# Layer 3 of a four-layer network: the shared expert's output held aside, the gathers taken by quarters, and the side work beside the first half's experts traced at twice the pace

## The chip, the cores and the metric

The kernel runs on one core of one Trainium2 chip. The metric is the time of one execution in microseconds (us). Profiles come from the hardware profiler; its engines are PE (TensorE matmul), PEld (TensorE weight load), DVE (VectorE), ACT (ScalarE), POOL (GpSimd) and SP (SyncE, which here only starts DMAs). Lines such as L1305 are line numbers of the kernel before.

## The reference

A network of four layers works on `x` of shape 4 x 1024 x 128 in fp32. Every layer is a mixer and a feed-forward part, each with a residual and a layer norm:

```python
x = _layernorm(x + _L3_attn_ref(x, ...), axis=-1)
x = _layernorm(x + _L3_ffn_ref(x, ...), axis=-1)
return x
```

Layers 0 to 2 (a gated scan and a quantized linear, a state space model and 16 experts, causal attention and 8 low-rank experts) are not touched. In layer 3 the mixer is a gated unit whose Toeplitz product runs over the first axis of `x`, which is 4 long, so a token mixes only with the tokens at the same place of the other three sequences. The feed-forward part of layer 3 is what this case is about:

```python
scores = softmax(flat @ router_w.T + router_bias)          # 32 experts
topk_scores, topk_idx = top_k(scores, 4)
topk_scores = topk_scores / clip(topk_scores.sum(-1), 1e-12)
h = silu(flat @ gate_w[e]) * (flat @ up_w[e])              # 128 wide, each expert e
sel = (h @ down_w[e])                                      # the four chosen experts
out = (sel * topk_scores).sum(1)
out = out + (silu(flat @ sgate_w.T) * (flat @ sup_w.T)) @ sdown_w.T   # shared, 512 wide
```

The shared expert reads the same input as the routed ones, and both sums are added to that input before the last norm.

## The kernel before

**Layout and parts.** `x` stays in SBUF as 32 tiles of 128 tokens x 128 features. Time is cut into four quarters; a quarter is 8 tiles (two of each of the 4 sequences). Layer 3 works on three parts: a is the quarters 0 and 1 (16 tiles), b is quarter 2, c is quarter 3 (8 tiles each). `xT` holds the same tokens turned, with features on the partitions.

**The chain of one part.** `l3_attn` (L1556) is the mixer: projections on PE, SiLU on ACT, the Toeplitz steps on DVE, the norm, and at its end `xT`. `l3_route` (L1656) computes the logits, the top 4 and the weights, a long row of small DVE steps; `positions` (L1239) turns them into a place in a list sorted by expert (`posl3a`, `posl3b`, `posl3c`, made at L1280) and the experts of the list's tiles. `spread` (L1317) is the **scatter**: for each tile of tokens four indirect DMAs, issued by POOL at L1305, write the rows of `x` into the list in HBM (`l3ra`, `l3rb`, `l3rc`): 64 for a, 32 for b, 32 for c. `l3_shared` (L1677) is the shared expert: per block of four tiles it makes four GLU chunks (two matmuls of `xT`, SiLU, product) and the down projection, and then DVE adds the result from PSUM to `x` at L1693. Part a has four blocks, b and c two each.

`small_experts` (L1705) runs the routed experts over the sorted list in groups of four list tiles, 20 groups for a and 12 each for b and c. A group is: a load `xg` by SP (L1336), which waits for all scatters of the part; PE transposes into `tp`; gate and up matmuls `gu` with the weights of the tile's expert; SiLU on ACT (L1735); the product `hg` on DVE (L1736); transposes and a DVE copy to `hT` (L169); the down matmuls; a copy `yg` from PSUM on ACT (L1750); and a store by SP to the list of outputs (`l3ya`, `l3yb`, `l3yc`). After the last group stands a branch (`rest_of`, L1358) for lists that are longer than the planned size; every engine passes it, and with this input its body is skipped.

`collect` (L1385) is the **gather**: for each tile of tokens four indirect DMAs (again POOL at L1305) fetch the outputs of its four experts into a buffer `yt`, and DVE adds them, weighted, to `x` (L1396). `yt` has 8 buffers of one tile, so the ninth tile's gather waits for the adds of the first. `finish` (L1788) norms a quarter (L185) and stores it with four DMAs of SP. The last part goes through `close` (L1863), which does this two tiles at a time.

**What orders the work.** Engines take their instructions in the order in which the program was traced, and the order is written by hand with generators in `all` (L1874). `chain` runs generators in turn, `abreast` side by side by their listed costs. `mix(main, side, pace)` (L241) traces a step of the main work, then as much of the side work as its cost allows; the side's instructions are put behind the main ones on their engine:

```python
            due += got[0]
            while due > 0.0:
                took = self.queued(side)
                due = 0.0 if took is None else due - took[0] * pace
```

So a pace of 0.75 lets the side advance by 1/0.75 of the main work's listed time. `press` (L1850) traces the side alone until a name is listed. The shared expert may not write to `x` before the part's scatter has read it, so `l3_shared` asserts that the scatter is listed. The end of the kernel (L1925 to L1945) makes one side chain `on`, in which the mixer and route of b, the scatter of b, the gathers and norms of a, the mixer and route of c, the scatter of c and the gathers and norm of b follow, and beside it:

```python
self.run(self.mix(self.chain(self.l3_shared(a, sw), self.l3_experts(a, wall3)), on, 0.75, False))
self.press(on, listed("l3b"))
self.run(self.mix(self.chain(self.l3_shared(b, sw), self.l3_experts(b, wall3)), on, 0.75, False))
self.press(on, listed("l3c"))
self.run(self.mix(self.chain(self.l3_shared(c, sw), self.l3_experts(c, wall3)), on))
self.run(self.close(c, yp))
```

In POOL's order this gives: the branch behind the experts of a, 32 scatters of b, 64 gathers of a, the branch behind the experts of b, 32 scatters of c, 32 gathers of b, the branch behind the experts of c, 32 gathers of c.

Of the kernel before, what the change touches and what calls it, by code (L numbers as in the profile page):

```python
# [20 lines left out]
P = 128  # L21
# [48 lines left out]
def tile_of(b, i):  # L70

    return i // 2 * QT + b * 2 + i % 2


class Kernel:
# [1598 lines left out]
            yield from self.positions(cp, "l3" + part.name, mask, w, part.nt, E3, K3)  # L1674
            yield (10.0,)

    def l3_shared(self, part, sw):  # L1677

        nc, x = self.nc, self.x
        NC = FS3 // P  # L1680
        with ExitStack() as c2:
            hp = self.pool(c2, "l3sh" + part.name, 2)
            ps = self.pool(c2, "l3sp" + part.name, 2, space=PSUM)
            assert "l3" + part.name in self.listed
            wd = sw[:, 2, :].rearrange("p (c d) -> p c d", d=D)
            for blk in range(part.t0 // 4, (part.t0 + part.nt) // 4):
                h = self.tile(hp, [P, NC, BLK], "hs", bufs=1)
                for c in range(NC):
                    f = slice(c * P, (c + 1) * P)
                    self.glu(ps, hp, h[:, c, :], sw[:, 0, f], sw[:, 1, f], blk)  # L1690
                py = self.down(ps, h, wd, NC)
                s = slice(blk * 4, blk * 4 + 4)
                nc.vector.tensor_tensor(x[:, s, :], py, x[:, s, :], ALU.add)  # L1693
                yield (9.0,)

    def l3_wall(self, ctx, right=False):
# [88 lines left out]
    def l3_experts(self, part, wall):  # L1785
        return self.small_experts("l3", E3, part, wall)

    def finish(self, part):  # L1788

        for q in range(part.q0, part.q0 + part.nq):  # L1790
            self.norm(self.quarter(q))
            yield (5.0,)
            for b in range(B):
                t = tile_of(b, 2 * q)
                self.nc.sync.dma_start(
                    out=self.out[b, q * TQ : (q + 1) * TQ, :].rearrange("(k p) d -> p k d", p=P),
                    in_=self.x[:, t : t + 2, :],
                )
            yield (1.0,)

    def chain(self, *gens):
        for g in gens:
# [53 lines left out]
        yield from self.l2_route(part)  # L1856
        yield from self.spread("l2", part, K2)

    def last(self, part, yp):
        yield from self.collect("l3", part, K3, yp)  # L1860
        yield from self.finish(part)

    def close(self, part, yp):  # L1863

# [9 lines left out]
    def all(self):  # L1874
# [4 lines left out]
        with ExitStack() as ctx:  # L1879
            lgp = self.pool(ctx, "l2lg")  # L1880
            self.l2_lg = self.tile(lgp, [P, NT, E2], "lg")
            with ExitStack() as early:

                self.l0_setup(early)
                self.l2_wr = self.load(lgp, self.ins["l2_wr"])
                self.run(self.l0_attn((0, 1)))
                self.l1_setup()
                self.l2_setup()
                self.zero_lists("l1")
                self.run(self.l0_ffn((0, 1)))  # L1890
                self.run(self.l1_attn((0, 1)))

                self.run(self.l1_route(a))
                self.run(self.mix(self.l0_attn((2, 3), True), self.spread("l1", a, K1)))
                self.zero_lists("l2", "l3")
                with ExitStack() as c2:
                    wall = self.l1_wall(c2)
                    yp = self.pool(c2, "l1ya", 5, right=True)
                    side = self.chain(self.l0_ffn((2, 3), True), self.l1_attn((2, 3), True))
                    self.run(self.mix(self.chain(self.l1_shared(a), self.l1_experts(a, wall)), side, 2.0, False))  # L1900
                    self.run(self.mix(self.abreast(self.l2_weights(), side), self.l1_close(a, yp)))
            with ExitStack() as c2:
                wall = self.l1_wall(c2)
                self.run(self.mix(self.l2_attn(0), self.chain(self.l1_route(r), self.spread("l1", r, K1))))
                wall2 = self.l2_wall(c2)
                yp = self.pool(c2, "l1yr", 5, right=True)
                self.run(self.mix(self.chain(self.l1_experts(r, wall), self.l1_shared(r)), self.routed(a2)))
                self.run(self.mix(self.l2_experts(a2, wall2), self.l1_close(r, yp)))
            listed = lambda name: lambda: name in self.listed
            on = self.served(  # L1910
                self.chain(self.rows_in(a2), self.onward(a, True)),
                (lambda: self.rows_done >= B + 2, self.routed(m2)),
                (lambda: self.rows_done == 2 * B, self.routed(n2)),
            )
            self.run(self.mix(self.l2_attn(1), on, drain=False))
            with ExitStack() as c3:
                with ExitStack() as c2:
                    wall = self.l2_wall(c2)
                    self.press(on, listed("l2m"))
                    self.run(self.mix(self.l2_experts(m2, wall), on, drain=False))  # L1920
                    self.press(on, lambda: {"l2n", "routed l3a"} <= self.listed)
                    sw, wall3 = self.l3_wall(c3, True)
                    on = self.chain(on, self.rows_in(m2))
                    self.run(self.mix(self.l2_experts(n2, wall), on, drain=False))
                self.press(on, listed("l3a"))  # L1925
                yp = self.pool(c3, "l3y", 8)

                on = self.chain(
                    on, self.collect("l2", n2, K2, yp, which=(0, 1, 4, 5)),
                    self.abreast(  # L1930
                        self.chain(self.l3_attn(b), self.l3_route(b)),
                        self.collect("l2", n2, K2, yp, which=(2, 3, 6, 7)),
                    ),
                    self.abreast(
                        self.chain(self.spread("l3", b, K3), self.when(listed("made l3a")), self.last(a, yp)),
                        self.chain(self.l3_attn(c), self.l3_route(c)),
                    ),
                    self.spread("l3", c, K3), self.when(listed("made l3b")), self.last(b, yp),
                )
                self.run(self.mix(self.chain(self.l3_shared(a, sw), self.l3_experts(a, wall3)), on, 0.75, False))  # L1940
                self.press(on, listed("l3b"))
                self.run(self.mix(self.chain(self.l3_shared(b, sw), self.l3_experts(b, wall3)), on, 0.75, False))
                self.press(on, listed("l3c"))
                self.run(self.mix(self.chain(self.l3_shared(c, sw), self.l3_experts(c, wall3)), on))
                self.run(self.close(c, yp))  # L1945
        bad = self.nc.values_load(self.flag[0:1, 0:1], min_val=0, max_val=1)
        with self.tc.If(bad > 0):  # L1947
            with ExitStack() as ctx:
# [9 lines left out]
                for p in self.parts:  # L1958
                    self.run(self.onward(p))
                    with ExitStack() as c2:  # L1960
                        sw, wall = self.l3_wall(c2)
                        self.run(self.l3_shared(p, sw), self.l3_experts(p, wall))
                        self.run(self.last(p, self.pool(c2, "l3y" + p.name, 5)))


@with_exitstack
# [162 lines left out]
```

## Time and profile before

| what | value |
|---|---|
| runs | 2449.0, 2435.38, 2435.16, 2447.52, 2448.98 us; median 2447.52 |
| the profiled execution | 2442.41 us, its span 2440.6 us |
| busy PE, PEld | 1603.6 us (66%), 955.2 us (39%) |
| busy DVE, ACT | 1270.5 us (52%), 803.3 us (33%) |
| busy POOL | 768.3 us (31%) |
| DMA | 187.10 MB, mean 77 GB/s |
| queue q0, which carries the indirect DMAs | 42.86 MB, 5.6% of the DMA engines' time |
| mean granted TensorE clock | 0.821 |

The span is the time from the first to the last record of the profiled execution; all stamps below are us from its start. Busy times are sums over the whole span, and they are far from full on every engine, so they do not say what sets the end. For that one cuts the span into stretches and looks at what each engine does in each. Layer 3's experts fill the last fifth: the experts of a begin at about 1942, and the last record is at 2440.6. A row of a group of instructions reads: line, engine, operation, output <- inputs, count, then the shortest, mean and longest duration in ns or the busy time, and the first and last start.

### The profile page before, as it was taken

The numbers are of one execution on the slowest core, as the hardware profiler recorded it, in microseconds if no ns is written. First come the engines' busy times: TensorE is split into PE (matmuls) and PEld (weight loads), VectorE is DVE, ScalarE is ACT, GpSimd is POOL, SyncE is SP. The second block draws the span as 40 slices with busy tenths as digits, with TensorE's granted clock in tenths as the row PEclk, the third lists the DMA queues.
The fourth block names the chain that finished last, engine by engine and source line by source line (L and its number), as shares of the span: only waits on it lengthen the run. The fifth ranks groups of instructions, "written<-read, shape, count | busy, mean of one in ns | idle before, by whom it ended". The sixth has DMA issues, their size and how long they took to land. (4 is left out here: it accounts for less than half of the span.)

```text
span 2440.6 us, 27065 instructions
## 1 busy us (share of the span) xinstructions
PE 1603.6 (66%) x9017; PEld 955.2 (39%) x9017; DVE 1270.5 (52%) x3630; ACT 803.3 (33%) x1159; POOL 768.3 (31%) x701
## 2 busy tenths in 40 slices
PE   7535776976571675586969787877726798262480
PEld 3214433843230335544623232344514485152270
DVE  8767795655670564324535675473602275252352
ACT  5511372322240332222336564542201164030140
POOL 5531285145227002234132002002372102727504
PEclk9766788988785898888979998888868899686695
DMA  9930002334201014312130000021411141131232
GB/s 308 288 104 0 12 36 80 117 110 152 77 28 52 17 57 155 100 50 62 43 104 21 1 1 17 2 113 39 159 71 33 43 123 53 51 99 61 67 100 59
DMA packets 215530, 187.10 MB, mean 77 GB/s; under 512 B 16528, under 2 KB 194064, under 8 KB 214864
## 3 DMA queue, kind: packets, MB, share of 16 engines
q1 hardware_dynamic: 194672, 142.29, 18.4%
q0 software_dynamic: 20704, 42.86, 5.6%
q8 instruction: 84, 1.38, 0.2%
q14 instruction: 70, 0.57, 0.1%
HBM read 88.49 MB, written 96.60 MB: 76 GB/s over the span
## 5 line engine op out<-in xcount | busy, mean ns | idle before, releaser
L1059 ACT ACTIVATE pr<-sc 128x1024 f32<-128x1024 f32 x288 | 279.6, 1021 | 321.5 <-PE sc L157 189.7
L157 PE MATMUL sc<-qm,kT 32*128 32x512 f32 (+3 forms) x1536 | 198.2, 559 | 21.7 <-ACT pr L1059 21.4
L157 PE MATMUL gu<-ld,xgT 128*128 x640 | 167.5, 406 | 60.1 <-issue 36.2
L157 PE MATMUL s<-pr,va 128*32 128x512 f32 (+3 forms) x1536 | 175.1, 523 | 46.1 <-issue 26.3
L165 PE MATMUL tp<-ld,hg 128*128 128x128 f32 x624 | 100.5, 282 | 102.5 <-DVE hg L1736 36.7
L157 PE MATMUL gu<-wall,xgT 128*128 x304 | 155.4, 637 | 2.9 <-ACT xgT L167 2.0
L157 PEld LDWEIGHTS gu<-ld,xgT 128*128 128x128 f32 x640 | 121.5, 201 | 86.3 <-issue 45.5
L1065 DVE TENSOR_TENSOR pr<-pr,ld 128x512 f32<-128x512 f32 (+1 forms) x160 | 92.1, 580 | 104.8 <-ACT pr L1059 101.7
L169 DVE COPY hT<-tp 128x512 f32<-128x512 f32 x118 | 80.8, 685 | 122.6 <-remote 64.8
L165 PEld LDWEIGHTS tp<-ld,hg 128*128 128x128 f32 x624 | 79.0, 145 | 155.4 <-issue 58.7
L157 PEld LDWEIGHTS sc<-qm,kT 32*128 32x128 f32 x1536 | 85.2, 198 | 120.5 <-issue 66.3
L1736 DVE TENSOR_TENSOR hg<-sg,gu 128x256 f32<-128x256 f32 x160 | 65.6, 416 | 127.9 <-ACT sg L1735 107.0
L167 ACT COPY xgT<-tp 128x512 f32<-128x512 f32 x99 | 57.9, 586 | 220.1 <-PE tp L165 155.2
L1305 POOL DMA_INDIRECT l1ra<-x,posl1a x64 | 93.3, 1458 | 61.2 <-DVE posl1a L1280 42.0
L1502 ACT ACTIVATE sg<-gu 128x512 f32<-128x512 f32 x76 | 45.4, 598 | 198.7 <-PE gu L157 126.0
L165 PE MATMUL tp<-ld,xg 128*128 128x128 f32 x396 | 65.0, 292 | 67.4 <-ACT hT L167 26.0
L1735 ACT ACTIVATE sg<-gu 128x256 f32<-128x256 f32 x160 | 60.8, 384 | 140.2 <-PE gu L157 69.0
L1305 POOL DMA_INDIRECT yt<-l1yr,posl1r x64 | 60.6, 947 | 142.8 <-DVE x L1396 83.2
L157 PEld LDWEIGHTS s<-pr,va 128*32 128x32 f32 x1536 | 38.6, 112 | 154.7 <-issue 108.0
L1504 DVE TENSOR_TENSOR hg<-sg,gu 128x512 f32<-128x512 f32 x76 | 51.7, 681 | 82.7 <-ACT sg L1502 65.0
L1305 POOL DMA_INDIRECT l1rr<-x,posl1r x64 | 62.2, 972 | 96.8 <-DVE posl1r L1280 77.6
L1305 POOL DMA_INDIRECT yt<-l1ya,posl1a x64 | 69.8, 1091 | 70.2 <-DVE x L1396 29.6
(441 smaller groups left out, 3516.1 us busy)
## 6 DMA issues: line engine op xcount, KB each, us to landing
wall<-wall SPq DMA_DIRECT2D x16, 768.0 KB
l3ra<-zero SPq DMA_DIRECT2D x1, 6144.0 KB
ld<-in_l_w SPq DMA_DIRECT2D x2, 3072.0 KB
wall<-we SPq DMA_DIRECT2D x24, 256.0 KB
ld<-in_l_w SPq DMA_DIRECT2D x1, 6144.0 KB
l1ra<-zero SPq DMA_DIRECT2D x1, 5120.0 KB
l1rr<-zero SPq DMA_DIRECT2D x1, 5120.0 KB
xg<-l3ra SPq DMA_DIRECT2D x20, 256.0 KB
```

What stands on the lines that cost most here:

```text
L157: return self.nc.tensor.matmul(out, lhsT, rhs, start=start, stop=stop)
L165: nc.tensor.transpose(pt[:, k * P : (k + 1) * P], s, self.ident)
L167: nc.scalar.copy(dst, pt[:, : n * P])
L169: nc.vector.tensor_copy(dst, pt[:, : n * P])
L1059: nc.scalar.activation(pr, sc[h], AF.Exp)
L1065: nc.vector.tensor_tensor(d, d, cst["tril"].unsqueeze(1).unsqueeze(1).to_broadcast([P, 2, n, P]), ALU.mult)
L1305: ins = self.nc.gpsimd.indirect_dma_start(**kw)
L1502: nc.scalar.activation(sg, gu[:, 0, :], AF.Silu)
L1504: nc.vector.tensor_tensor(h, sg, gu[:, 1, :], ALU.mult)
L1735: nc.scalar.activation(sg, pg[:, :, 0, :], AF.Silu)
L1736: nc.vector.tensor_tensor(h[:, 2 * c : 2 * c + 2, :], sg, pg[:, :, 1, :], ALU.mult)
```

## The change

- **Shared output held.** For b and c, `l3_shared` gets a tile `sh` of 8 x 128 columns. ACT copies each block's result from PSUM into it, and the add to `x` is one DVE instruction over all 1024 columns, traced after the experts of the part. Since `x` is not written before that, the shared expert may stand ahead of the scatter: it now starts when the mixer's `xT` is listed (`mixed l3b`, `mixed l3c`), with the rest of the route and the scatter traced beside it, and only the experts wait for the scatter to be listed.
- **Gathers by quarters.** `finish` and `last` take one quarter. The gathers and the norm of a's first quarter stay beside the mixer and route of c; those of its second quarter move behind the scatter of c, ahead of the gathers of b.
- **Pace.** Beside the shared expert and experts of a the pace goes from 0.75 to 0.5, so the side advances by 2 units per unit of the main work. Beside the experts of c it goes from 1 to 0.75; what is left of the side is traced at the end of that, as before.

The gathers of c and `close` stay as they are. `l3_shared` for a still adds each block to `x` at once. The number of indirect DMAs and the matmuls are the same. In POOL's order the change gives: 12 scatters of b, the branch behind the experts of a, 20 scatters of b, 32 gathers of a, the branch behind the experts of b, 32 scatters of c, 32 gathers of a, the branch behind the experts of c, 32 gathers of b, 32 gathers of c.

```diff
--- before.py
+++ after.py
@@ -1674,14 +1674,18 @@
             yield from self.positions(cp, "l3" + part.name, mask, w, part.nt, E3, K3)
             yield (10.0,)
 
-    def l3_shared(self, part, sw):
+    def mark(self, name):
+        self.listed.add(name)
+        yield (0.0,)
+
+    def l3_shared(self, part, sw, sh=None):
 
         nc, x = self.nc, self.x
         NC = FS3 // P
         with ExitStack() as c2:
             hp = self.pool(c2, "l3sh" + part.name, 2)
             ps = self.pool(c2, "l3sp" + part.name, 2, space=PSUM)
-            assert "l3" + part.name in self.listed
+            assert sh is not None or "l3" + part.name in self.listed
             wd = sw[:, 2, :].rearrange("p (c d) -> p c d", d=D)
             for blk in range(part.t0 // 4, (part.t0 + part.nt) // 4):
                 h = self.tile(hp, [P, NC, BLK], "hs", bufs=1)
@@ -1689,8 +1693,12 @@
                     f = slice(c * P, (c + 1) * P)
                     self.glu(ps, hp, h[:, c, :], sw[:, 0, f], sw[:, 1, f], blk)
                 py = self.down(ps, h, wd, NC)
-                s = slice(blk * 4, blk * 4 + 4)
-                nc.vector.tensor_tensor(x[:, s, :], py, x[:, s, :], ALU.add)
+                if sh is None:
+                    s = slice(blk * 4, blk * 4 + 4)
+                    nc.vector.tensor_tensor(x[:, s, :], py, x[:, s, :], ALU.add)
+                else:
+                    t = blk * 4 - part.t0
+                    nc.scalar.copy(sh[:, t : t + 4, :], py)
                 yield (9.0,)
 
     def l3_wall(self, ctx, right=False):
@@ -1785,18 +1793,17 @@
     def l3_experts(self, part, wall):
         return self.small_experts("l3", E3, part, wall)
 
-    def finish(self, part):
-
-        for q in range(part.q0, part.q0 + part.nq):
-            self.norm(self.quarter(q))
-            yield (5.0,)
-            for b in range(B):
-                t = tile_of(b, 2 * q)
-                self.nc.sync.dma_start(
-                    out=self.out[b, q * TQ : (q + 1) * TQ, :].rearrange("(k p) d -> p k d", p=P),
-                    in_=self.x[:, t : t + 2, :],
-                )
-            yield (1.0,)
+    def finish(self, q):
+
+        self.norm(self.quarter(q))
+        yield (5.0,)
+        for b in range(B):
+            t = tile_of(b, 2 * q)
+            self.nc.sync.dma_start(
+                out=self.out[b, q * TQ : (q + 1) * TQ, :].rearrange("(k p) d -> p k d", p=P),
+                in_=self.x[:, t : t + 2, :],
+            )
+        yield (1.0,)
 
     def chain(self, *gens):
         for g in gens:
@@ -1856,9 +1863,10 @@
         yield from self.l2_route(part)
         yield from self.spread("l2", part, K2)
 
-    def last(self, part, yp):
-        yield from self.collect("l3", part, K3, yp)
-        yield from self.finish(part)
+    def last(self, part, yp, q=0):
+
+        yield from self.collect("l3", part, K3, yp, q * QT, QT)
+        yield from self.finish(part.q0 + q)
 
     def close(self, part, yp):
 
@@ -1928,20 +1936,25 @@
                 on = self.chain(
                     on, self.collect("l2", n2, K2, yp, which=(0, 1, 4, 5)),
                     self.abreast(
-                        self.chain(self.l3_attn(b), self.l3_route(b)),
+                        self.chain(self.l3_attn(b), self.mark("mixed l3b"), self.l3_route(b)),
                         self.collect("l2", n2, K2, yp, which=(2, 3, 6, 7)),
                     ),
                     self.abreast(
-                        self.chain(self.spread("l3", b, K3), self.when(listed("made l3a")), self.last(a, yp)),
-                        self.chain(self.l3_attn(c), self.l3_route(c)),
+                        self.chain(self.spread("l3", b, K3), self.when(listed("made l3a")), self.last(a, yp, 0)),
+                        self.chain(self.l3_attn(c), self.mark("mixed l3c"), self.l3_route(c)),
                     ),
-                    self.spread("l3", c, K3), self.when(listed("made l3b")), self.last(b, yp),
+                    self.spread("l3", c, K3), self.last(a, yp, 1), self.when(listed("made l3b")), self.last(b, yp),
                 )
-                self.run(self.mix(self.chain(self.l3_shared(a, sw), self.l3_experts(a, wall3)), on, 0.75, False))
-                self.press(on, listed("l3b"))
-                self.run(self.mix(self.chain(self.l3_shared(b, sw), self.l3_experts(b, wall3)), on, 0.75, False))
-                self.press(on, listed("l3c"))
-                self.run(self.mix(self.chain(self.l3_shared(c, sw), self.l3_experts(c, wall3)), on))
+                self.run(self.mix(self.chain(self.l3_shared(a, sw), self.l3_experts(a, wall3)), on, 0.5, False))
+                hold = self.pool(c3, "l3hold", 2)
+                for p in (b, c):
+                    self.press(on, listed("mixed l3" + p.name))
+                    sh = self.tile(hold, [P, QT, D], "sh")
+                    self.run(self.mix(self.l3_shared(p, sw, sh), on, 0.75, False))
+                    self.press(on, listed("l3" + p.name))
+                    self.run(self.mix(self.l3_experts(p, wall3), on, 0.75, p is c))
+                    s = slice(p.t0, p.t0 + QT)
+                    self.nc.vector.tensor_tensor(self.x[:, s, :], sh, self.x[:, s, :], ALU.add)
                 self.run(self.close(c, yp))
         bad = self.nc.values_load(self.flag[0:1, 0:1], min_val=0, max_val=1)
         with self.tc.If(bad > 0):
```

The slow general path behind a flag, which isn't taken here, calls `last` once for each quarter.

## The prediction

> **What bounds the kernel now.** I read the slices of the page first. In the last quarter the TensorE digits fall to 1 and 2 where POOL's are 5 to 7. So I asked for the busy times of the stages of layer 3, in this order: experts of part a; shared and scatter of b; experts of b; shared of c; experts of c; the close. Columns: stretch, length, then busy time and count of PE, PEld, DVE, ACT, POOL, then granted clock, DMA share, GB/s.
>
> ```profile
> 1942.00:2041.00 99.00, 89.59 (x560) 76.90 (x560) 64.28 (x208) 63.40 (x128) 0.00 (x0) 0.98 0.35 106
> 2041.00:2146.00 105.00, 43.45 (x143) 25.13 (x143) 34.27 (x104) 11.84 (x20) 62.98 (x64) 0.69 0.16 49
> 2146.00:2273.00 127.00, 60.57 (x331) 51.58 (x331) 54.39 (x207) 33.41 (x65) 62.26 (x64) 0.72 0.27 81
> 2273.00:2334.00 61.00, 30.06 (x96) 15.65 (x96) 15.27 (x59) 9.12 (x13) 30.35 (x32) 0.67 0.22 60
> 2334.00:2384.00 50.00, 45.55 (x288) 40.55 (x288) 30.00 (x93) 26.87 (x52) 0.00 (x0) 0.97 0.41 125
> 2384.00:2440.00 56.00, 0.00 (x0) 0.00 (x0) 16.85 (x60) 1.44 (x5) 30.18 (x32) 0.51 0.19 52
> ```
>
> Where POOL has no indirect DMA, PE is busy for 90% of the time. In the three stages with indirect DMAs it is busy for 41 to 49%, and no other engine is full. The views of the tiles give POOL's order there (first and last start):
>
> ```profile
> L1305 POOL DMA_INDIRECT l3rb<-x,posl3b x32: 954/958/1949, 2053.2 to 2094.4; - x32
> L1305 POOL DMA_INDIRECT yt<-l3ya,posl3a x64: 938/944/1086, 2095.6 to 2216.4; - x64
> L1305 POOL DMA_INDIRECT l3rc<-x,posl3c x32: 954/958/1761, 2217.6 to 2257.9; - x32
> L1305 POOL DMA_INDIRECT yt<-l3yb,posl3b x32: 940/944/1014, 2274.9 to 2313.8; - x32
> L1336 SPq DMA_DIRECT2D xg<-l3rc x12: 359/360/501, 2331.2 to 2363.2; - x12
> L1305 POOL DMA_INDIRECT yt<-l3yc,posl3c x32: 940/944/947, 2386.7 to 2425.4; - x32
> ```
>
> Part c's scatter stands behind all 64 gathers of a, though its positions (`posl3c`, L1280) were made at 2205.2. The waits of 2095 to 2145 show what a burst of indirect DMAs does:
>
> ```profile
> DVE x L1693 <- remote: 47.7, 1, 47.7
> PEld s L157 <- issue: 30.8, 13, 2.6
> PE s L157 <- issue: 30.7, 14, 2.5
> ```
>
> PE waits for nothing that the profile shows, yet starts one matmul in 2.5 us; DVE stands for 47.7 us at an add whose matmuls ended at 2103. By 20 us slices, 2120 to 2140 has 8 matmuls and no DVE or ACT instruction, 2300 to 2320 two and none. So back-to-back indirect DMAs stop the other engines. They don't stop at once: PE went on for 19 us after the start of the burst at 2053.2, 15 after 2274.9, 12 after 1886.6. I call this the grace. After a burst ends it takes 5.6 us (2314.7 to 2320.3) until DVE goes on. When POOL's gathers are spaced by waits, as between 2162 and 2189, PE keeps working. **The tail is therefore POOL's bursts and the experts mostly in turn**, and what counts is their order. The view of the DMAs from 2095 to 2145 lists no packet of the two instruction queues; the cause of the stop it doesn't tell.
>
> [...]
>
> **The change, part by part.** All times are on the clock of the profiled execution (span 2440.6, 1.8 us around it, 2442.4 in all; the runs shown have a median of 2447.5, 5 above it). The instructions of the changed program, engine by engine, give POOL's new order: 12 scatters of b, the branch after experts a, 20 scatters of b, 32 gathers of a's first quarter, scatter c, 32 gathers of a's second quarter, gathers of b, gathers of c. The number of indirect DMAs is the same.
>
> *Pace 0.5 beside experts a.* Route b's positions now come with three expert groups of a left; before, they came at 2052.2, after all. DVE takes on the rest of route b and the start of c's attention, some 20 us of work (2039 to 2060 in the trace, with other work between). It had 35 us free of 99, and PE gets only some 2 us more. So the stage, 2040.4 at its end, grows by 0 to 20; I take 7, nearer the row with free time: 2047. With 4.9 us a group (98 us for 20), the first scatter starts at 2047 - 15 + 1 = 2033, 20 earlier. The last groups of a (14 us) fit into the grace, and their lists are in memory by 2048, long before the gathers of a start at 2074.
>
> *First burst.* 64 indirect DMAs took 82.2 us (2053.2 to 2135.4): now 2033 to 2115. Shared b had 8 us ahead of the burst and the grace; now it starts 14 us into the burst. In the stopped part (2072 to 2139) PE got 54 matmuls through; shared b has 96, so some 30 are left for after it, 6 us more than before. The first transposes of experts b came 11.3 us after the burst (2146.7); now 2115 + 11 + 6 gives 2132, and I take 2133 (2126 if shared b is done, 2146 if half of its 21 us is left).
>
> *Shared output held.* L1693 on b and c, four adds of 0.69 us on DVE, becomes four ACT copies (0.59 each, as L1750) and two adds of 1024 columns (L1957); no row has this form, and by two of 0.69 each they cost 2.8 in all, the same (0 to 6). ACT is idle there. The add for b waits for all scatters of b; behind it on DVE stand c's toeplitz steps and the products of experts b, which need those scatters anyway. What goes is the stall of L1693 on scatter b (11.7 us), inside the burst: nothing by itself.
>
> *Experts b without a burst.* Before, 8 of 12 groups took 42 us (2147 to 2189) beside c's attention, its route and spaced gathers: 5.3 each. Now all 12 run so: 64 us, to 2197 (43 us if each took 3.54 as in experts c, so 2176; 78 at 6.5, so 2211). POOL is idle meanwhile. Positions of c come just after the branch behind experts b, so scatter c starts at 2201, not 2217.7.
>
> *Scatter c and second half of a.* 41.2 us, to 2242. Five of the eight tile buffers are free by then, so 20 gathers follow without a pause, 25 us, to 2267. Restart 5.6: 2273. Shared c runs beside this as it did beside the gathers of b: it got as far as the middle of its second block in the grace, and 9.5 us were left (2321.7 to 2331.2). So it ends at 2283, and 3 us later (xg issue to first transposes, 2331.2 to 2334.2) experts c start at 2286; before, 2334.2. If the grace covers it, 2279. On SP's queue four stores of a's quarter now stand between the third and the fourth load for experts c; they wait for a's norm, which DVE does ahead of the first products anyway: 0, up to 5.
>
> *Experts c.* 48 us (2334.2 to 2382.0), to 2334. The eight gathers left of a take 10 us, in the grace. DVE adds a's 32 rows between, as it added b's before: same cover.
>
> *Gathers of b, what is late next.* They were over at 2314.7, 72 us before they could matter. Now each tile waits for an add of a, the first behind 7 groups: 2286 + 4 + 7 x 3.54 = 2315. 32 gathers take 39.8 us: 2355, and a pause for the last buffers, 6 (0 to 26, if the last groups of experts c fall outside the grace): 2361. The gathers of c follow. From their first start to the end of the span was 2440.6 - 2386.7 = 53.9.
>
> **Sum:** 2361 + 54 = 2415 of span, 25 less than 2440.6 (rounded); with the 1.8, **2417**. Low end: experts a not longer (-7), shared b done in the burst (-6), experts b at 4.4 a group (-11), shared c in the grace (-7), no pause (-6): 2380. High end: experts a +13, experts b +14, pause +16: 2460.
>
> **Rivals.**
> 1. *Larger gain.* The grace starts anew in POOL's small pauses, so shared b and c and the ends of experts b and c lose little. For it: from 2162 to 2189, with 13 indirect DMAs, PE was busy for 24 of 27 us. Against: the bursts at 2223 and 2290 stopped all. Half of the low end's terms: 2399; all: 2380.
> 2. *The first half's pace gives nothing.* Experts a drag by 20 us, since the long chain of route b stands in DVE's order ahead of the products, and experts b take 6.5 a group. Then only the new place of scatter c pays: 2417 + 13 + 14 = 2444.
> 3. *Slower: no grace, strict turns.* For it: PE stopped at 2190.5, 8 us after 12 gathers began at 2182.7. Scatter b then stops experts a with three groups left: scatter to 2074, restart and groups to 2094, gathers to 2134, restart and shared b (two blocks of 10.4, 1919.3 to 1929.8 in shared a) to 2161, experts b 2164 to 2228, scatter c and 20 gathers from 2231 to 2297, restart and shared c to 2324, the eight gathers and a restart to 2343, experts c to 2391, gathers of b, no longer out of the way, to 2431, end 2485: 2487. It decides once the gathers of c start after 2399, 12 us later than before.
>
> **How the numbers follow.** Forecast (2402 to 2430) 0.46; larger gain (2370 to 2402) 0.18; rival 2 (2430 to 2454) 0.22; slower 0.14. A measurement of this kernel can tell about 0.5%, 12 us, from no change. Faster by more: 0.46 + 0.18 = 0.64; within: 0.22; slower by more: 0.14. The range 2380 to 2460 leaves out some 0.07 below and 0.12 above.
>
> **What would show it.** First l3rb scatter at 2033; first transposes of experts b near 2133, of experts c near 2286; `posl3c` near 2200; gathers of b inside experts c; gathers of c from 2361. If experts a end after 2060, the first step is wrong; if experts b take 78 us, the fourth; if PE works through the 66 us from scatter c on, my reading of the bursts is. A first gather of c after 2387 means that nothing was won.

## The result and the profile after

The changed kernel took 2455.76 us (median of 42 runs, 2436.43 to 2469.71), the kernel before 2443.54 us (median of 79). The ratio is 1.0046, 95% interval [1.0033, 1.0059]: slower by 11 to 12 us, less than the 0.5% that the text on record called the limit of one measurement, but clear of zero over so many runs. The forecast was 2417 us, a gain of 25.

The profiled execution took 2471.81 us (span 2469.8), 16 above the median of the runs. First the busy times of its stretches of layer 3, cut where its own stages change (columns as before: stretch, length, then busy time and count of PE, PEld, DVE, ACT, POOL, clock, DMA share, GB/s):

```profile
2080.00:2098.00 18.00, 0.00 (x0) 0.00 (x0) 0.00 (x0) 0.58 (x1) 11.39 (x13) 0.50 0.16 57
2098.00:2135.00 37.00, 13.53 (x20) 4.95 (x20) 2.07 (x3) 5.02 (x7) 27.24 (x29) 0.59 0.20 54
2135.00:2160.00 25.00, 21.88 (x89) 13.55 (x90) 11.92 (x27) 5.72 (x10) 0.00 (x0) 0.80 0.00 1
2160.00:2220.00 60.00, 56.56 (x356) 48.20 (x354) 41.73 (x142) 35.37 (x69) 0.00 (x0) 0.97 0.32 98
2225.00:2306.00 81.00, 28.93 (x97) 17.40 (x95) 16.38 (x53) 5.36 (x9) 61.39 (x64) 0.65 0.16 51
2316.00:2350.00 34.00, 30.38 (x183) 27.04 (x184) 15.81 (x37) 18.52 (x36) 0.00 (x0) 0.90 0.50 147
2350.00:2380.00 30.00, 11.94 (x67) 10.38 (x65) 8.40 (x26) 2.92 (x7) 22.73 (x24) 0.72 0.26 69
2404.00:2470.00 66.00, 0.00 (x0) 0.00 (x0) 26.52 (x102) 1.48 (x5) 30.63 (x32) 0.50 0.20 56
```

The stretches are cut at the ends of the bursts, and they alternate: where POOL has its indirect DMAs PE has 0 to 40% of the time, where POOL has none PE has 88 to 94%. (In the last stretch PE has no work left.) The experts of b (2160 to 2220) now run without an indirect DMA beside them and take 60 us. The views of the tiles of the same kernel give POOL's order:

```profile
L1305 POOL DMA_INDIRECT l3rb<-x,posl3b x32: 954/958/1236, 2050.0 to 2089.8; - x32
L1305 POOL DMA_INDIRECT yt<-l3ya,posl3a x64: 940/944/1030, 2094.0 to 2305.5; - x64
L1305 POOL DMA_INDIRECT l3rc<-x,posl3c x32: 954/958/1479, 2225.4 to 2265.4; - x32
L1305 POOL DMA_INDIRECT yt<-l3yb,posl3b x32: 940/944/1097, 2350.2 to 2402.8; - x32
L1305 POOL DMA_INDIRECT yt<-l3yc,posl3c x32: 940/944/1047, 2404.1 to 2443.3; - x32
```

The gathers of c begin at 2404.1; in the kernel before they began at 2386.7. The waits of 2060 to 2135 (engine, tile and line, releaser: us in all, times, longest) show what stands still beside scatter b and the first gathers:

```profile
PE s L165 <- issue: 35.2, 2, 21.6
DVE hs L744 <- remote: 29.5, 1, 29.5
ACT yg L1758 <- remote: 15.1, 1, 15.1
```

`yg` at L1758 is a group of the experts of a: its last two stores, which the forecast had inside the grace, left at 2072.1 and 2090.6, while scatter b ran from 2050.0 to 2089.8.

### The profile page after: what moved, and what is told of

It is laid out like the page before. It is cut to its first block, busy times and chain, and to the rows that moved or that the text cites. A ratio compares the mean times of both kernels' runs of the same rounds, so it can differ in the third digit from the quotient of the medians.

```text
span 2469.8 us, 27062 instructions
## 1 busy us (share of the span) xinstructions
PE 1606.3 (65%) x9017; PEld 957.8 (39%) x9017; DVE 1274.5 (52%) x3628; ACT 804.0 (33%) x1161; POOL 769.1 (31%) x701
## 5 line engine op out<-in xcount | busy, mean ns | idle before, releaser
L744 DVE TENSOR_TENSOR hs<-sg,pu 128x512 f32<-128x512 f32 x48 | 32.7, 685 | 121.9 <-remote 74.0
L165 PEld LDWEIGHTS tp<-ld,xg 128*128 128x128 f32 x396 | 49.8, 152 | 115.5 <-issue 48.2
```

Of the source, the lines that this page charges most:

```text
L165: nc.tensor.transpose(pt[:, k * P : (k + 1) * P], s, self.ident)
L744: nc.vector.tensor_tensor(dst, sg, pu, ALU.mult)
```

## The experiments

The runs fell on different chips, and these are of two kinds. On the first kind, that of the result, the kernel before takes 2430 to 2444 us; on the second it takes 2032 to 2036. Ratios are against the kernel before on the same chip. On the second kind the kernel before has times but no profile. In a stretch where POOL has nothing to do the two kinds run alike: from the first to the last store of the experts of a the kernel before takes 84.6 us on the first kind, and the quarters alone, the same program up to there, 84.6 on the second. All kernels of this table compute the same thing as the kernel before.

| kernel | first kind: ratio, interval | second kind: ratio, interval |
|---|---|---|
| the whole change | 1.0046 [1.0033, 1.0059]; again 1.0037 [1.0018, 1.0056] | 0.9945 [0.9922, 0.9968] |
| pace 0.5 alone | 1.0008 [0.9988, 1.0028] | 0.9915 [0.9897, 0.9934] |
| quarters alone | 1.0032 [1.0013, 1.0050] | 0.9939 [0.9914, 0.9963] |
| held output alone | 1.0010 [0.9982, 1.0038] | 1.0221 [1.0203, 1.0239] |
| held and quarters, pace 0.75 | not run | 1.0357 [1.0339, 1.0375] |
| before, spaced by 512 columns | 0.9712 [0.9670, 0.9754] | not run |
| before, spaced by 128 columns | not run | 1.0075 [1.0047, 1.0103] |
| pace 0.5, spaced by 512 | not run | 1.0216 [1.0181, 1.0252] |
| whole change, spaced by 512 | not run | 1.0203 [1.0172, 1.0234]; again 1.0198 [1.0160, 1.0236] |
| whole change, spaced by 128 | not run | 0.9994 [0.9978, 1.0011] |
| before, all layers spaced by 320 | not run | 1.0332 [1.0297, 1.0367] |

### One part at a time, second kind of chip

Edits: the pace alone (`0.75` to `0.5` in the line of the experts of a); the quarters alone (`finish`, `last` and the side chain of the change, the shared output added at once); the held output alone (`sh`, `mark` and the loop over b and c, with `self.last(a, yp, 0), self.last(a, yp, 1)` in one place; the loop brings the pace of 0.75 beside the experts of c with it); all but the pace of 0.5.

> The kernel before with one edit: the pace beside the shared expert and experts of a is 0.5. Theory A (the loss of the whole change comes from the dragged end of the experts of a, whose last groups fall into the burst of scatter b): last store of l3ya near 2090 instead of 2041, first transposes of the experts of b near 2162 instead of 2147, and a time 10 to 20 us above that of the kernel before. Theory B (the loss comes from the gathers of b that now stand ahead of those of c): the pace alone costs nothing, within 5 us of the kernel before.

> The kernel before with the gathers of a in two quarters, the second behind the scatter of c, at the old pace of 0.75 and 1; the shared output is added at once as before. Theory A: the first transposes of the experts of b stay near 2147, the experts of b take about 60 us, the scatter of c starts near 2210; gathers of b stop the last groups of the experts of c, so what was won is given back: within 7 us of the kernel before. Theory B: 10 us or more slower than the kernel before.

> The kernel before with the shared output of b and c held and added after the experts, the shared expert starting when the mixer's part is done; all gathers of a in one piece as before, pace 0.75 beside the experts of a. Theory A: shared b gains its 8 us ahead of the scatter at most, shared c runs beside the scatter of c and not beside the gathers of b, and the experts of c start when the gathers of b are over, near 2320 instead of 2334: 8 to 16 us faster than the kernel before. Theory B says nothing against it; if the held tile and its late add cost by themselves, it is no faster.

> The changed kernel with the pace beside the experts of a back at 0.75. Theory A: the experts of a end near 2041 again, the experts of b start 12 to 16 us earlier than in the changed kernel, and the time is 10 to 20 us below it, at or a little below the kernel before. Theory B: as slow as the changed kernel, 8 to 16 us above the kernel before.

The time of 2033 us came unlooked for, and theories A and B, whose numbers were for the first kind, both miss here. The pace and the quarters gained 0.85% and 0.6%, the held output lost 2.2%, and with the quarters 3.6%. Of the waits of the last kernel from scatter b to the end of the experts of b (1765 to 1913) these bear on the loss:

```profile
ACT sg L1743 <- PE gu L157: 44.8, 14, 27.7
DVE x L1396 <- DMA yt<-l3ya,posl3a: 30.9, 4, 28.4
DVE x L1957 <- DMA l3rb<-x,posl3b: 30.5, 1, 30.5
```

The add of the held output, written after the experts, stands on DVE ahead of their products, and waits 30.5 us for the scatters of b. That wait ends at 1808.1, when the list of the experts of b is complete, so it holds back c's mixer, which stands behind it, and not the experts. Inside the experts DVE then waits 28.4 us, to 1848.8, at an add of a gathered tile that stands ahead of their next products. The experts of b took 100 us there instead of the 65 of the quarters alone. At the pace of 0.75 shared b, which now goes first, also pushes route b back: `posl3b` comes 242 us after `posl3a`, with the quarters alone 231. The held output alone has the same two waits (30.5 and 28.5 us).

### The change and the kernel before, profiled side by side; a measuring block

> The changed kernel as it is, on the chip of the experiments, where the kernel before takes 2033 us and not 2444. If the held output is what costs there (the kernels with it took 1.022 and 1.036 of the time before, those without it 0.992 and 0.994), 1.02 to 1.04; if the pace of 0.5 and the held output need one another, 0.98 to 1.00.

> The kernel before, for its profile on the chip of the experiments. If the difference of 400 us comes from bursts of indirect DMAs that do not stop the other engines here, PE, DVE and ACT go on at more than half their pace in the stretches of scatter b and of the gathers of a and b, and stretches without indirect DMAs take as long as before.

> The kernel before with a measuring block behind its last store, outputs unchanged: first DVE, ACT and PE streams without waits and 40 turns of DVE and ACT with no indirect DMA; then the streams beside a burst of 64 gathers; then the turns beside such a burst; then the turns beside 64 gathers with a memset of 512 columns on POOL between them. Where bursts stop the others by slow signals between engines, the streams run at full pace in the second part and a turn takes 5 us or more in the third; where by instruction supply, the streams slow down too; where they do not stop them, all parts but for a few per cent take as long as the first. The fourth shows whether spacing changes it.

These three fell on a chip of the first kind. The changed kernel gave 1.0037 and a second profile (span 2446.5), nearer to its median than the first. The kernel before gave a span of 2444.1, with the stages of its first profile within 5 us. In the probe (streams are instructions without waits, a turn is one DVE instruction and one of ACT that wait for each other) the scheduler moved the turns ahead: 66 of the 120 had run before the second burst, 54 ran beside it, and the spaced burst had nothing beside it, so it says nothing. The busy times of the first stretch (streams, no DMA) and of the second (the same streams beside 64 gathers, after its first 9 us):

```profile
2431.00:2446.00 15.00, 15.00 (x117) 15.00 (x118) 15.00 (x146) 14.58 (x100) 0.00 (x0) 0.87 0.04 12
2465.00:2537.00 72.00, 11.30 (x31) 8.14 (x30) 11.43 (x61) 6.83 (x40) 54.31 (x59) 0.53 0.18 52
```

```profile
L157 PE MATMUL pm<-src x31: 270/371/565, 2464.8 to 2536.0; 128*128 128x128 f32 x31
L157 PEld LDWEIGHTS pm<-src x30: 186/288/288, 2465.1 to 2533.9; 128*128 128x128 f32 x30
  issue: 121.2, 58
```

Without indirect DMAs PE, DVE and ACT are full, with 117 matmuls in 15 us; beside them PE does 31 in 72 us. The last row is PE's idle time, matmuls and weight loads together: 58 waits, none of them for anything that the profile names. So for these streams a burst of indirect DMAs is neither a late signal nor a late transfer of their data: they start instructions more slowly. The text on record had asked for this if the supply of instructions is what suffers, but the probe doesn't tell that from any other cause of slow starts. Beside the second burst 54 turns of DVE and ACT, all that were left, went through in its first 36 us. So here too the stop did not come at once; how long this grace would have lasted is not known.

### One part at a time, first kind of chip

> The pace of 0.5 alone again, for a chip where the kernel before takes 2440 us. Theory C (indirect DMAs in a burst and the other engines work strictly in turn there, so that only their sum and the waits between them count): the scatter of b starts some 20 us earlier, the last two groups of the experts of a are stopped until it ends, the experts of b start near 2147 as before, and the time stays within 6 us of the kernel before. Theory A: 10 to 20 us slower.

> The quarters alone again, for a chip where the kernel before takes 2440 us. Theory C: the experts of b end near 2208 instead of 2271, but the gathers of b leave the stretch beside shared c and stop the last five groups of the experts of c; shared c stands behind a burst of 72 indirect DMAs and one of 32 follows inside the experts of c: 15 to 35 us slower than the kernel before. If the gathers are covered by the experts, faster by 10 us or more.

> The held shared output alone again, for a chip where the kernel before takes 2440 us. Theory C: shared c is done before the gathers of b, which stand in a burst as before, so the experts of c start near 2320 instead of 2334: 5 to 15 us faster than the kernel before. If the late add, which waits on DVE for all scatters of b, holds up what stands behind it (as on the other chip, where it waited 30.5 us and the kernel was 1.022 of the time before): 10 us or more slower.

Theory C got the pace right, and the direction of the quarters, not their size (7 us instead of 15 to 35). The held output gained nothing, where theory C had 5 to 15 us. All four kernels have moved the middle of the stage and not the first gather of c. Times in us after `posl3a` was made, which takes out what the layers ahead vary by:

| kernel | first scatter of b | first load for experts b | first scatter of c | first load for experts c | first gather of c | end |
|---|---|---|---|---|---|---|
| before | 313 | 404 | 478 | 591 | 647 | 701 |
| pace alone | 292 | 404 | 484 | 586 | 644 | 698 |
| quarters alone | 311 | 401 | 451 | 566 | 650 | 704 |
| held alone | 324 | 367 | 497 | 565 | 646 | 699 |
| whole change (second profile) | 295 | 404 | 469 | 559 | 648 | 713 |

The first load for the experts of c comes 5 to 32 us earlier than before, the first gather of c within 3 us of that of the kernel before in all. From there to the end each part alone takes 54 us, as before, and the whole change 65. The held output alone shows how it is lost, in its stretches from scatter c to the end of the experts of c:

```profile
2233.00:2302.00 69.00, 23.01 (x89) 12.67 (x87) 24.17 (x82) 6.24 (x10) 42.26 (x38) 0.69 0.12 43
2302.00:2335.00 33.00, 14.21 (x56) 10.97 (x56) 2.70 (x6) 4.96 (x9) 24.87 (x27) 0.71 0.36 103
2335.00:2382.00 47.00, 36.16 (x232) 32.87 (x232) 27.66 (x88) 22.27 (x43) 0.48 (x1) 0.86 0.35 105
```

The experts of c have their list at 2302, but the gathers of b run until 2335 and PE does 56 matmuls beside them; the other 232 follow in 47 us. In these kernels, on this kind of chip, bursts and matmuls work mostly in turn, and putting one ahead of the other moved nothing.

### Spacing the DMAs

```python
         self.moved = self.moved[-130:] + [ins.ins.name]
+        if self.spaced:
+            f = self.nc.gpsimd.memset(self.fill, 0.0)
+            self.tc.add_manual_dep(f.ins, ins.ins.name, behind, reason="queued behind")
+            self.moved.append(f.ins.name)
```

> The kernel before with a memset of 512 columns on POOL behind each indirect DMA of this last stage but for the gathers of c: one DMA in 1.66 us instead of 1.25. It computes the same. If the others stop because a queue fills up at one DMA in 1.25 us and drains a little more slowly, spacing sets them free: the experts of b start near 2110 instead of 2147, those of c near 2300 instead of 2334, and the time falls by 20 to 40 us. If each indirect DMA costs the others a fixed time, nothing is won and the bursts take 0.4 us more for each of 160: 20 to 60 us slower.

It took 2360.05 us against 2429.64: 0.9712 [0.9670, 0.9754], and more than the 20 to 40 us that were expected. So the stop hangs on how closely the DMAs follow one another and is no fixed cost of each; what stops the engines this doesn't tell. Two of its tiles, its stretches, and one of the kernel before (the last row):

```profile
L1306 POOL DMA_INDIRECT l3rb<-x,posl3b x32: 964/965/1276, 2016.1 to 2069.7; - x32
L1306 POOL DMA_INDIRECT yt<-l3yc,posl3c x32: 940/944/1003, 2305.8 to 2344.5; - x32
```

```profile
2072.00:2120.00 48.00, 40.27 (x242) 35.09 (x242) 30.96 (x118) 25.84 (x51) 43.28 (x59) 0.90 0.49 138
2120.00:2140.00 20.00, 0.00 (x0) 0.00 (x0) 0.00 (x0) 0.00 (x0) 18.05 (x25) 0.57 0.19 56
...
2235.00:2290.00 55.00, 39.18 (x224) 34.26 (x224) 23.42 (x67) 19.37 (x40) 48.29 (x64) 0.81 0.46 130
```

```profile
2275.00:2315.00 40.00, 18.97 (x57) 8.95 (x55) 9.54 (x43) 7.33 (x10) 30.27 (x32) 0.67 0.29 78
```

From 2072 to 2120 POOL issues some 29 DMAs and as many memsets, and PE is busy for 40 of 48 us beside them; before, at 1.25 us a DMA, PE was busy for 19 of the 40 us beside the gathers of b, most of them in the grace. 32 scatters take 55 us instead of 42, yet the first gather of c comes 573 us after `posl3a` instead of 647. Some 30 of these 74 us are won ahead of scatter b, since the edit also spaces the last gathers of layer 2, beside shared a: the first store of the experts of a comes 187 us after `posl3a` instead of 217. What is left are waits that the profile can name: from 2120 to 2140 all but POOL stand still behind one add on DVE, which waits 24.6 us for gathers of a.

> The changed kernel with the same memset of 512 columns behind each indirect DMA but those of the gathers of c. It computes the same. Theory C (only the stops took the gain of the change): with the stops gone the change shows its worth, and this is faster than the spaced kernel before, under 2350 us where that took 2360. Theory D (the change costs by itself: the held add waits on DVE for all scatters of b with the products of the experts queued behind it, and the gathers of b stand between the experts of c and the gathers of c): 2375 to 2430 us.

> The pace of 0.5 alone, with the spacing. With the stops gone the earlier route of b should pay as it did on the chip without stops (0.992 of the time before): about 2340 us. If the dragged experts of a cost as much as the earlier scatter wins: 2360.

> The kernel before with a memset of only 128 columns behind each indirect DMA, about 1.35 us a DMA. If the stops follow from a queue that drains a little more slowly than one DMA in 1.25 us, this is between: 2380 to 2430 us, with a longer run of work before each stop. If any pause on POOL's queue sets the others free, 2355 or less, since it costs less than the longer memset.

> The kernel before with a memset of 320 columns behind each indirect DMA of all layers but the gathers of c. If the bursts of layers 1 to 3 ahead of the last stage stop the other engines too (between 1780 and 1825 PE has no or few matmuls beside the scatter of a): 20 to 60 us faster than the 2360 of the kernel spaced in the last stage alone. If those bursts stand alone on the path, 0.3 us for each of them is lost: 2360 to 2420.

These fell on the second kind, so they don't answer what was asked of the first. There the spaced forms are slower, the more so the longer the pause: 0.75% for 128 columns (1.35 us a DMA by the estimate on record), 2.0 to 2.2% for 1.67 us with the change or the pace, 3.3% in all layers. Whether 128 columns are enough on the first kind, and whether layers 1 and 2 gain from spacing there, is open.

> The changed kernel with the memset of 512 columns behind each indirect DMA, again, for a chip where the kernel before takes 2440 us; there the kernel before with the same spacing took 0.971 of the time before. Theory C (only the stops took the gain of the change): under 0.967. Theory D (the change costs by itself, as on the chip without stops, where its spaced form took 1.020): 0.98 to 1.00.

> The changed kernel as it is, beside it. On a chip where the kernel before takes 2440 us: 1.004 again. On one where it takes 2033 us, theory D: 1.01 to 1.03, since the held output without the pace took 1.036 there; theory C: below 0.99, since nothing stops the other engines there.

> The changed kernel with a memset of 128 columns behind each indirect DMA but those of the gathers of c: one DMA in 1.35 us. On a chip where the kernel before takes 2440 us, if a rate a little below one DMA in 1.26 us sets the other engines free and the change has its worth there as on the chip without stops (0.9945 of the time before): 2350 to 2385 us, the experts of b without a gap and no stretch of 10 us without an instruction of PE; if 1.35 us is still too fast, the stops stay and the time is 2400 to 2450. On a chip where it takes 2033 us: between the changed kernel without spacing (0.9945) and with the larger memset (1.020), 1.00 to 1.01, by 160 times 0.08 us of POOL time.

Again the second kind. The changed kernel as it is took 0.9945 there: it is worth 0.55% where bursts don't stop the others, less than the pace alone (0.9915, on another chip of that kind). That is less than theory C asked for (below 0.99) and the other sign from theory D. With the pace of 0.5 the add of the held output (L1957) starts at 1776.2, after the scatter of b (1732.1 to 1772.4), DVE stands 0.3 us ahead of it instead of 30.5, and no add of a gathered tile holds DVE up in the experts of b. So the price of the held output hangs on the pace beside it. Its stretches of scatter b, experts b, scatter c, experts c, gathers of b and gathers of c:

```profile
1732.00:1774.00 42.00, 35.53 (x152) 22.43 (x151) 24.27 (x72) 18.94 (x34) 32.11 (x33) 0.88 0.24 84
1774.00:1837.00 63.00, 58.54 (x370) 49.97 (x369) 44.64 (x153) 35.84 (x69) 32.77 (x32) 0.97 0.48 132
1841.00:1883.00 42.00, 21.95 (x96) 13.51 (x94) 15.62 (x53) 7.53 (x12) 31.99 (x33) 0.78 0.13 50
1883.00:1935.00 52.00, 45.97 (x288) 41.13 (x288) 30.35 (x86) 25.09 (x50) 39.59 (x41) 0.92 0.64 177
1935.00:1964.00 29.00, 0.00 (x0) 0.00 (x0) 16.01 (x63) 2.35 (x3) 21.91 (x24) 0.52 0.33 84
1964.00:2018.00 54.00, 0.00 (x0) 0.00 (x0) 19.58 (x73) 1.48 (x5) 30.07 (x32) 0.50 0.23 61
```

Beside 33 unspaced scatters 152 matmuls go through, and beside 41 unspaced gathers the experts of c do all their 288. From scatter c on POOL is the bound here: from the first scatter of c at 1841.3 to the last gather of c at 2003.5 it issues 128 DMAs in 162 us, one in 1.27 us, and the experts of c are done 29 us before the gathers of b. That is the place where a transfer that was out of the way before now stands on the path. With the larger memset the same queue took 200 us (1854.3 to 2054.1), 38 us more, and the first scatter of c came 336 us after `posl3a` instead of 323; together that is about what the spaced form of the change loses against it (2.6%). With 128 columns the gain and the loss cancelled.

## Why the prediction was wrong

The reading of the bottleneck held: bursts and the other engines work mostly in turn. What failed is that the forecast still let work overlap the bursts, shared b in the first one and the last groups of the experts of c beside the gathers of b, and took over the close as it was. The sum came out 38 us too small in the second profile, where 25 were forecast as the gain. In us after `posl3a`, with the forecast's stamps less 1739.9, where the profile of before has it:

| step | forecast | before | after, first profile | after, second profile |
|---|---|---|---|---|
| first scatter of b | 293 | 313 | 305 | 295 |
| last store of experts a | 307 | 301 | 345 | 334 |
| first gather of a | 334 | 356 | 349 | 338 |
| first load for experts b | 390 | 404 | 414 | 404 |
| first scatter of c | 461 | 478 | 480 | 469 |
| first load for experts c | 543 | 591 | 570 | 559 |
| first gather of b | 575 | 535 | 605 | 594 |
| first gather of c | 621 | 647 | 659 | 648 |
| end | 675 | 701 | 724 | 713 |

The second profile departs from the forecast by 14 us up to the first load for the experts of b, by -6 from there to the first scatter of c, by 8 to the first load for the experts of c, by 3 to the first gather of b, by 8 to the first gather of c and by 11 to the end: 38 in all.

- **Pace 0.5 beside experts a: right for scatter b, wrong for the experts.** The scatter came where forecast (295 for 293); the first profile was 10 us late in shared a already. "The last groups of a fit into the grace" failed: the last two groups were stopped until scatter b was nearly over. It cost only 4 us in the end, since the first gathers of a wait for that scatter anyway.
- **First burst: failed.** The forecast let 66 of the 96 matmuls of shared b through. The last groups of a used up the grace, 20 matmuls of all kinds went through from 2098 to 2135, and shared b was done after the burst. The experts of b start 14 us later than forecast, exactly where they did before. So the earlier scatter won nothing, as the pace alone shows (404 in both).
- **Shared output held: right on this kind of chip that the add costs nothing by itself** (1.0010), though why is not shown. On the other kind it costs 2.2% alone, at the pace of 0.75. There the sentence that what stands behind the add on DVE needs those scatters anyway fails: c's mixer stands there and doesn't need them, and an add of a gathered tile stands ahead of the products of the experts.
- **Experts b without a burst: right.** 60 us for 12 groups (64 forecast), and 65 us from their first load to the first scatter of c (71 forecast).
- **Scatter c and second half of a: mis-sized.** 20 gathers were to follow without a pause, since five buffers were thought free; all 32 did, 64 indirect DMAs in 81 us. From the first scatter of c to the start of the experts of c this took 8 us more than forecast, but they start still 32 us earlier than in the kernel before.
- **Gathers of b: the step that gave the gain back.** The forecast started them at 575, behind the seventh group, and gave 46 us to the first gather of c. They took 54, since the last five groups of the experts of c, stopped beside them, had to run in a pause of their own (67 matmuls from 2350 to 2380, 40 from 2380 to 2404). The lead of 32 us at the start of the experts of c became nothing at the first gather of c.
- **The close: taken over as 54, took 65.** The adds of the last tiles of b, the norm of b's quarter and its stores now stand on DVE beside the gathers of c: 102 instructions of DVE in the last stretch, where the kernel before has 60. From 2410 to 2440 DVE gets 31 of them through, and 56 are left when the last gather is over; before, 12 were. So c's own adds and norms end 11 us later.

From the first profile's rows the third rival was the nearest in mechanism: strict turns, with the experts of a stopped, and the gathers of b "no longer out of the way". Its point of decision, a first gather of c after 2399, was passed in the first profile (2404.1), which was 10 us late in shared a already, and not in the second (2381.2; 648 us after `posl3a` against 647 before). Its price of 44 us was almost four times too high. The forecast's error was to count each shift as a gain where, with engines that work mostly in turn, only the sum of the turns counts; the three parts and the whole change with one first gather of c agree with that. The changed kernel was not run with spaced DMAs on the first kind, so whether it would gain there without the stops is not shown.

What stays open is why the engines slow down on the first kind of chip. The rate of the DMAs matters (one in 1.25 us against one in 1.67), and it is no wait for data, since streams without waits slow down too (in the probe 31 matmuls in 72 us, against 117 in 15). The supply of instructions stays a rival that no run decides: from 2070 to 2156 the kernel before shows no packet of the two instruction queues (84 and 70 packets in the whole run), and the changed kernel on the second kind shows four beside gathers of a (1773 to 1806), but its engines also did far more work there (370 matmuls of PE from 1774 to 1837, against 85 from 2060 to 2135 in the kernel before), and no view tells whether an engine waited for a packet. One more difference was seen: the profiles of the first kind give no landing time for transfers and name many releasers only "remote", those of the second kind give landing times and no "remote". The wall loads of a chip of each kind, the first from the kernel after and the second from the same kernel:

```profile
wall<-wall SPq DMA_DIRECT2D x16, 768.0 KB
```

```profile
wall<-wall SPq DMA_DIRECT2D x16, 768.0 KB, 7.3
```

The profiles of the first kind thus lack something that those of the second have. No run here shows whether this bears on the stops, or whether the engines stop when nothing is recorded.

## What to carry to other kernels

Before counting a shift as a gain, ask whether the two things that now overlap can run at once: on the first kind of chip one scatter or gather in 1.25 us and the other engines mostly could not, and four orders of the same work (the kernel before and each part alone) ended within 6 us of each other. Where back-to-back indirect DMAs and idle engines without a named wait stand in the same stretch, try spacing the DMAs first: a memset of 0.54 us behind each took 2.9% off the kernel there, more than any order, while the spaced forms that ran on the other kind were up to 3.3% slower or no faster. And measure on more than one chip: the same change was 0.5% slower on one kind and 0.55% faster on the other.

## What the runs showed of the hardware

- Chips differ: the kernel before takes 2430 to 2444 us on those of the result and on two of the experiments, and 2032 to 2036 on three others. For the changed kernel some 214 us of the difference lie behind `posl3a` (713 against 499 us), as much again ahead of it (spans of 2446.5 and 2017.8 us), where layers 1 and 2 have bursts of indirect DMAs too; what those cost on the first kind was not measured.
- On the first kind a burst at 1.25 us a DMA leaves PE 31 matmuls in 72 us in the probe, after a grace of 8 to 19 us; with a DMA and a memset in turn, one DMA in 1.67 us, PE is busy for 40 of 48 us.
- A DVE instruction that is written behind a loop can stand ahead of its products in the engine's order, so the order in which the program was traced is not always the order that an engine gets. In the held output on the second kind such an add waited 30.5 us for scatters at the pace of 0.75, and 0.3 us at 0.5.
